# One graph-attention layer on one core: batches of eight tiles, E times Q made with features on partitions, and every edge tile gathered

## The chip, the cores and the metric

The kernel runs on one core of a Trainium2 chip. A core has five engines that each run their own queue of instructions in order: TensorE (PE: matmuls; PEld: its weight loads), VectorE (DVE), ScalarE (ACT), GpSimd (POOL) and SyncE (SP). They wait for each other through semaphores. SyncE starts the plain transfers between the device memory (HBM) and the on-chip memory (SBUF); GpSimd starts the indirect ones, which fetch rows by a list of indices. Results of TensorE go to PSUM, a small memory of eight banks, and are read from there by VectorE and ScalarE. The metric is device time in microseconds (us) of one execution. A short program on the host only lays the inputs out (transposed copies, padded index lists).

## The reference

There are 6250 nodes with 128 features, eight heads of 16 features, and 206,250 edges sorted by their destination node. For every edge e from `src` to `dst`:

```
Q = x @ WQ;  K = x @ WK;  V = x @ WV        # per node, 128 wide
E = edge_attr @ WE                          # per edge, 128 wide
score[e,h] = sum over the head's 16 features of K[src] * Q[dst] * E[e]
w[e,h]     = exp(clip(score / 4, -5, 5))
out[n]     = sum over edges into n of w * V[src]  /  (sum of w + 1e-6)
result     = layernorm(x + out)
```

Everything is float32. Three tensors meet in the score: K by a random source node, Q by a destination that hardly moves from edge to edge, and E by the edge itself.

## The kernel before

The edges are cut into 1612 tiles of 128. Four tiles make a batch (`B = 4`; a few smaller batches at the end).

**Tables.** `table` (from L256) computes K and V of all nodes as one row of 256 numbers and stores them to HBM (`kv`). `q_rows` (L284) makes Q as three bfloat16 parts and stores it (`qs`); `load_q` (L308) loads the 42 destination rows that a group of eight tiles can need. Until the table is stored, the first 12 batches (`XB`, 48 tiles) gather rows of x and `project` (L408) turns them into K and V: transposes, a copy, matmuls, copies.

**Gathers.** `gather` (L388) issues one indirect transfer per tile: 128 rows of 1 KB into `kvrows` (L397, GpSimd). There are 14 buffers of four tiles. From batch 18 on (`LOCK`) the first gather of a batch also waits for a matmul of TensorE several batches earlier (`lag`, `expanded`): the gathers are tied to TensorE's pace.

**Column tiles.** For two batches in five, from batch 32 on, the last tile is not gathered: 146 tiles in all (`column_tiles`, L74). `columns` (L352) copies, for each of the tile's 128 edges, one column of the transposed x (4 bytes on each of 128 partitions) into `xcol`, at an address that the engine loads into a register (L365, L370): 96 copies on ScalarE and 32 on VectorE per tile. `project_columns` (L372) multiplies the tile by the K and V weights and `place_columns` (L382) copies the result to where a gather would have put it.

**A batch's way.** `stage_a` (L457): TensorE expands Q of the destinations into `qps` with a one-hot matrix (L464: edges on the output's partitions, the one-hot is the stationary operand, so one weight load per tile), and multiplies the edge features with WE into `eps` (L469, again one weight load per tile). `stage_b` (L472): VectorE multiplies K by Q (L475), the product by E (L478), sums over 16 features (L481) and clips (L484). `weigh` (L487): ScalarE takes the exponential twice, into PSUM for the multiplication (L490, `exp_p`) and into the message (L492). `messages` (L517): VectorE multiplies V by the weights (L519). `stage_c` (L524): TensorE sums the messages into windows of nodes with a second one-hot (L541, `agg`); ScalarE copies finished windows out (L552), `finish` (L507) adds the windows of 256 nodes up (`finps`, L504), and `layernorm` (L735) runs in pieces on VectorE between other work (`fill`).

**Order.** One loop over the batches (L585) emits `stage_a` of batch b, `stage_b` of b-1, `messages` and `stage_c` of b-2. From batch 12 on that order is kept as written (a manual schedule); before that the framework's scheduler orders the instructions. SyncE's queue carries the edge features (`ea`, L334), the broadcast destinations (`relb`, L324), `qw`, `xb` and the results.

Of the kernel before, what the change touches and what calls it, by code (L numbers as in the profile page):

```python
# [16 lines left out]
P = 128  # L17
# [3 lines left out]
B = 4  # L21
G = 4
# [7 lines left out]
GB = 14  # L30
XB = 12
LOCK = XB + 6
STEP = 3
GLEAD = 2
OHB = 5
# [5 lines left out]
AHEAD = 2  # L41
EB = 6
SLAG = 2
# [8 lines left out]
COL0 = 32  # L52
COLP = (5, 2)
COLA = (8, 12)
COLV = (8, 4)
COLL = 8
RING = 4096
SUMS = 8
XT_AT = RING + P
# [3 lines left out]
def cut_batches():  # L63
    out, t = [], 0
    while t < NT:
        k = B
        if t >= NT - TAIL:
            k = 2 if NT - t > 3 else 1
        out.append(range(t, t + k))
        t += k  # L70
    return out


def column_tiles():  # L74

    batches = cut_batches()
    at = (COL0 + k * COLP[0] // COLP[1] for k in range(len(batches)))
    return [batches[b][-1] for b in at if b < len(batches) and batches[b][-1] < NT - TAIL - 4 * B]

# [22 lines left out]
def edge_attention(ctx: ExitStack, tc: tile.TileContext, x, xT, srcT, srcC, dstT, dstB, dst0, bnd, lo, eaT,  # L102
# [26 lines left out]
    onehots = [cp.tile([P, HW + 2 * B * P], F32, name=f"onehot{i}") for i in range(OHB)]  # L129
# [4 lines left out]
    col_batches = [t // B for t in column_tiles()]  # L134
    col_half = (len(col_batches) + 1) // 2
    col_at = cp.tile([col_half, 2, P], I32, name="col_at")
# [4 lines left out]
    with ExitStack() as fast:  # L141
# [80 lines left out]
        def count_inside():  # L222

            W = 4 * 2 * D
            for a in range(0, NT, W):
                e = min(NT, a + W)
                cl = wp.tile([P, W], F32, name="cl", tag="kvst", bufs=2)[:, :e - a]
                count(P, cl, rel[:, a:e], HW - 1)
            nc.vector.tensor_reduce(cn[:, :1], cn, axis=AX.X, op=ALU.add)
            pc = psT.tile([1, 1], F32, name="pc", tag="oT")  # L230
            nc.tensor.matmul(pc, cn[:, :1], ones, start=True, stop=True)
            nc.vector.tensor_copy(cnt_i, pc)
# [7 lines left out]
        psT = fast.enter_context(tc.tile_pool(name="psT", bufs=2, space=bass.MemoryType.PSUM))  # L240
        psA = fast.enter_context(tc.tile_pool(name="psA", bufs=2, space=bass.MemoryType.PSUM))
        psX = fast.enter_context(tc.tile_pool(name="psX", bufs=1, space=bass.MemoryType.PSUM))

        iota_p = psX.tile([P, HW], F32, name="iota_p")
        exp_p = psX.tile([P, B, H], F32, name="exp_p")
        nc.vector.tensor_copy(iota_p, iota_f[:, :HW])

        def pair_bank(i, name, shape):

            pool, tag = ((psE, "eps"), (psT, "oT"), (psQ, "qps"), (psT, "oT"))[i % 4]  # L250
# [33 lines left out]
        def q_rows(q):  # L284
            n = min(P, N - q * P)
            ps = psT.tile([P, D], F32, name="qrows", tag="oT")
# [40 lines left out]
        chunks, aggs, sums, st8, expanded = {}, {}, {}, {}, {}  # L327
# [15 lines left out]
        def lag(b):  # L343

            return max(STEP, 12 - (b - LOCK) // 40)

        col_tiles, xT_bytes = {}, xT_sb.bitcast(U8)
        used = [0]

        copied, projected = {}, []  # L350

        def columns(eng, b, share=1.0):  # L352

            size, runs = COLA if eng is nc.scalar else COLV
            first = 0 if eng is nc.scalar else COLA[0] * COLA[1]
            engine = mybir.EngineType.Activation if eng is nc.scalar else mybir.EngineType.DVE
            copy = eng.copy if eng is nc.scalar else eng.tensor_copy
            due = int((b - COL0 + COLL - 1 + share) * runs * COLP[1] / COLP[0] + 1e-6)
            while copied.get(engine, 0) < min(due, len(col_batches) * runs):
                k, j = divmod(copied.get(engine, 0), runs)  # L360
                copied[engine] = copied.get(engine, 0) + 1
                if k not in col_tiles:
                    col_tiles[k] = wp.tile([P, P], F32, name="xcol", bufs=4)
                to, j = col_tiles[k].bitcast(U8), first + j * size
                at = nc.values_load_multi_w_load_instructions(  # L365
                    col_at[k % col_half:k % col_half + 1, k // col_half, j:j + size], engines=(engine,),
                    min_val=XT_AT + 4 * LEFT, max_val=XT_AT + 4 * (LEFT + N - 1),
                    skip_runtime_bounds_check_because="edges name nodes")[1]
                for c in range(size):
                    copy(to[:, 4 * (j + c):4 * (j + c) + 4], xT_bytes[:, ds(at[c] - XT_AT, 4)])  # L370

        def project_columns(b):  # L372

            if b not in col_batches:
                return
            g = gathered[b]
            k = col_batches.index(b)
            pk = psT.tile([P, 2 * D], F32, name="colkv", tag="oT")
            nc.tensor.matmul(pk, col_tiles.pop(k), wkv_sb, start=True, stop=True)  # L379
            projected.append((g, pk))  # L380

        def place_columns():  # L382

            while projected:
                g, pk = projected.pop()
                nc.vector.tensor_copy(g[:, B - 1, :], pk)

        def gather(b, made=None):  # L388
            rows, f = (x, D) if b < XB else (kv, 2 * D)
            g = gp.tile([P, B, 2 * D], F32, name="kvrows")  # L390
            for i, t in enumerate(batches[b]):
                if b in col_batches and i == B - 1:
                    continue
# [6 lines left out]
                if i == 0 and b >= LOCK:  # L400
                    made = expanded[b - lag(b)]
# [6 lines left out]
        def project(g, n):  # L408

            pt = psT.tile([P, B, P], F32, name="xtps", tag="oT")  # L410
            for i in range(n):
                nc.tensor.transpose(pt[:, i, :], g[:, i, :D], ident)
            xgT = wp.tile([P, B, P], F32, name="xgT", tag="kq", bufs=2)
            nc.scalar.copy(xgT[:, :n], pt[:, :n])
            for i in range(0, n, 2):
                k = min(2, n - i)
                pk = pair_bank(i // 2, "kvps", [P, 2, 2 * D])
                for j in range(k):
                    nc.tensor.matmul(pk[:, j, :], xgT[:, i + j, :], wkv_sb, start=True, stop=True)  # L419
                nc.scalar.copy(g[:, i:i + k, :], pk[:, :k, :])  # L420

        def together(b):

            t0 = batches[b][0]
            n = len(batches[b])
            if n == B and b + 1 < nbat and len(batches[b + 1]) == B and t0 % (2 * B) == 0:
                return [b, b + 1]
            return [] if n == B and t0 % (2 * B) else [b]

        def stage_0(b):  # L430
            group = together(b)
            if not group:
                return
            t0, n = batches[b][0], sum(len(batches[i]) for i in group)
            tl = onehots[used[0] % OHB]
            used[0] += 1
# [3 lines left out]
            for i in group:  # L440
                st8[i] = tl, HW + (batches[i][0] - t0) * P - HW * pair_of(batches[i][0])[1], None

        def stage_0t(b):
            group = together(b)
            if not group:
                return
            t0, n = batches[b][0], sum(len(batches[i]) for i in group)
            ohT = wp.tile([QROWS, 2 * B * P], BF16, name="onehotT", bufs=3)
# [3 lines left out]
            for i in group:  # L452
                tl, at, _ = st8[i]
                k = (batches[i][0] - t0) * P
                st8[i] = (tl, at), ohT[:, k:k + len(batches[i]) * P]

        def stage_a(b, g):  # L457
            t0, n = batches[b][0], len(batches[b])
            if b < XB:
                project(g, n)  # L460
            oh, ohT = st8.pop(b)
            pq = psQ.tile([P, B, D], F32, name="qps")
            for i in range(n):
                expanded[b] = nc.tensor.matmul(pq[:, i, :], ohT[:, i * P:i * P + P], loaded[t0 // WT],  # L464
                                               start=True, stop=True)
            pe = psE.tile([P, B, D], F32, name="eps")
            ea = ea_tiles(t0, n)
            for i in range(n):
                nc.tensor.matmul(pe[:, i, :], ea[:, i * P:i * P + P], we_sb, start=True, stop=True)  # L469
            st8[b] = [n, g, oh, pq, pe]  # L470

        def stage_b(b):  # L472
            n, g, oh, pq, pe = st8[b]
            t0 = wp.tile([P, B, D], F32, name="kq", bufs=2)
            nc.vector.tensor_tensor(t0[:, :n], g[:, :n, :D], pq[:, :n], op=ALU.mult)  # L475
            yield
            t1 = wp.tile([P, B, D], F32, name="kqe", bufs=2)
            nc.vector.tensor_tensor(t1[:, :n], t0[:, :n], pe[:, :n], op=ALU.mult)  # L478
            yield
            sc = wp.tile([P, B, H], F32, name="sc")  # L480
            nc.vector.tensor_reduce(sc[:, :n], t1[:, :n].rearrange("p b (h d) -> p b h d", h=H),  # L481
# [3 lines left out]
            st8[b] = [n, g, oh, sc]  # L485
# [327 lines left out]
```

## Time and profile before

| | |
|---|---|
| three runs | 2565.03, 2586.32, 2592.5 us (median 2586.32) |
| the profiled execution | 2567.26 us, of which 2565.4 us are the span from its first to its last instruction |
| mean granted TensorE clock | 0.75 of full speed |
| busy: PE / PEld | 1624.0 us (63%) / 1407.1 us (55%) |
| busy: VectorE, ScalarE, GpSimd | 1843.5 us (72%), 1644.0 us (64%), 1396.9 us (54%) |
| indirect gathers | 1466 (48 from x, 1418 from `kv`) |
| DMA | 380.81 MB, mean 148 GB/s |

How to read the profile's rows: "L370 ACT COPY xcol<-xT_sb 128x4 uint8 x14016 | 1499.0, 189 | 573.0 <-issue 560.3" is a group of 14,016 copies of line 370 on ScalarE that write `xcol` from `xT_sb`; together they were busy for 1499.0 us, one lasts 189 ns (they overlap a little), and the engine stood idle for 573.0 us just before them, 560.3 of it while it waited for nothing that the profile shows ("issue"). In a timeline the first two numbers are start and duration in us, and the bracket is the idle time before. "remote" is a wait ended by a semaphore that the profile can't assign.

### The profile page before, as it was taken

To read this page: it belongs to the slowest core of one execution; us is meant where nothing else is said; L and a number is where in the kernel's file an instruction comes from. 1 tells how busy PE (TensorE), PEld (TensorE's weight loads), DVE (VectorE), ACT (ScalarE), POOL (GpSimd) and SP (SyncE) were. 2 spreads that over 40 slices of the span, in tenths; PEclk is the share of its full clock that TensorE was granted. 3 is DMA by queue.
4 is the path that set the end of the run, shared out by engine and by line. 5 is a ranking of instruction groups with operands and counts; after the bars stand their busy time and mean duration, and the time that the engine had idled before them with its cause. 6 is when DMAs were issued, how large, how long until landed. Compare 5 with 4: busy or idle time off the path is not lost.

```text
span 2565.4 us, 49832 instructions
## 1 busy us (share of the span) xinstructions
PE 1624.0 (63%) x9342; PEld 1407.1 (55%) x9342; DVE 1843.5 (72%) x8070; ACT 1644.0 (64%) x15015; POOL 1396.9 (54%) x1473
## 2 busy tenths in 40 slices
PE   5656566676666666666666655667666656566665
PEld 3446555565665555555555555556556555455555
DVE  2436678878777777777767777877877777777786
ACT  1211667777776677676767767777776666776760
POOL 6446555555555455555554555555655555555564
PEclk7777777777776777776777768777876777777787
DMA  7545445645554464455444544564654455545542
GB/s 233 153 130 179 136 125 157 176 134 169 153 148 132 134 176 138 123 147 174 130 135 136 175 140 129 147 175 137 183 147 126 136 144 164 145 131 144 173 145 79
DMA packets 171028, 380.81 MB, mean 148 GB/s; under 512 B 58653, under 2 KB 84569, under 8 KB 170707
## 3 DMA queue, kind: packets, MB, share of 16 engines
q0 software_dynamic: 69584, 189.03, 25.8%
q1 hardware_dynamic: 99983, 187.46, 24.4%
q14 instruction: 244, 2.00, 0.2%
q8 instruction: 77, 1.26, 0.2%
q10 hardware_dynamic: 1140, 1.06, 0.1%
HBM read 362.61 MB, written 14.81 MB: 147 GB/s over the span
## 4 chain that ended last, share of the span: by engine, by line
ACT 46%; issue 25%; DVE 11%; PE 8%; ACTq 6%; another core or an unknown queue 3%; DMA 1%; DVEq 0%; SPq 0%
ACT xcol L370 42%; ACTq L365 6%; DVE xcol L370 2%; PE agg L541 2%; PE eps L469 2%; ACT msg L492 2%; DVE kqe L478 2%; DVE msg L519 1%; DVE kq L475 1%; PE finps L504 1%; ACT exp_p L490 1%; PE kvps L419 1%; DVE sc L481 1%; ACT sum L552 1%
## 5 line engine op out<-in xcount | busy, mean ns | idle before, releaser
L397 POOL DMA_INDIRECT kvrows<-kv,src x1418 | 1350.3, 952 | 1120.4 <-PE qps L464 420.4
L370 ACT COPY xcol<-xT_sb 128x4 uint8 x14016 | 1499.0, 189 | 573.0 <-issue 560.3
L541 PE MATMUL agg<-msg,onehot 128*128 128x136 f32 x3224 | 639.1, 358 | 441.3 <-DVE msg L519 316.8
L541 PEld LDWEIGHTS agg<-msg,onehot 128*128 128x128 f32 x3224 | 562.4, 254 | 492.2 <-ACT msg L492 276.5
L469 PE MATMUL eps<-we_sb,ea 128*128 128x128 f32 x3224 | 599.6, 343 | 164.5 <-DVE kqe L478 95.3
L469 PEld LDWEIGHTS eps<-we_sb,ea 128*128 128x128 f32 x3224 | 517.8, 244 | 220.6 <-DVE kqe L478 128.7
L519 DVE TENSOR_TENSOR msg<-kvrows,exp_p 128x512 f32<-128x512 f32 x406 | 275.9, 679 | 488.8 <-ACT exp_p L490 276.4
L370 DVE COPY xcol<-xT_sb 128x4 uint8 x4672 | 410.9, 192 | 30.2 <-issue 23.0
L464 PE MATMUL qps<-qw,onehotT 126*128 126x128 bf16 x1612 | 193.5, 254 | 240.7 <-DVE kq L475 163.2
L464 PEld LDWEIGHTS <-onehotT 126*128 126x128 bf16 x1612 | 154.7, 117 | 325.3 <-issue 306.8
L478 DVE TENSOR_TENSOR kqe<-kq,eps 128x512 f32<-128x512 f32 x406 | 274.6, 676 | 52.3 <-remote 30.7
L475 DVE TENSOR_TENSOR kq<-kvrows,qps 128x512 f32<-128x512 f32 x406 | 273.7, 674 | 37.5 <-remote 21.3
L481 DVE TENSOR_REDUCE sc<-kqe 128x32 f32<-128x512 f32 x406 | 272.8, 672 | 5.8 <-DVE y L761 0.5
L490 ACT ACTIVATE exp_p<-sc 128x32 f32<-128x32 f32 x406 | 78.3, 193 | 139.7 <-DVE sc L484 76.8
L437 DVE TENSOR_TENSOR onehot<-iota_p,dst_sb 128x512 f32<-128x512 f32 (+2 forms) x206 | 137.6, 669 | 11.0 <-remote 9.0
L379 PE MATMUL colkv<-wkv_sb,xcol 128*128 128x256 f32 x292 | 127.9, 533 | 0.0
L504 PE MATMUL finps<-sum,shift 128*128 128x136 f32 x640 | 95.2, 310 | 17.1 <-ACT sum L552 11.1
L504 PEld LDWEIGHTS finps<-sum,shift 128*128 128x128 f32 x640 | 91.1, 219 | 19.6 <-ACT sum L552 13.1
L492 ACT ACTIVATE msg<-sc 128x32 f32<-128x32 f32 x406 | 87.2, 215 | 22.2 <-issue 21.7
L450 DVE TENSOR_SCALAR onehotT<-relb,node 126x1024 bf16<-126x1024 bf16 (+2 forms) x206 | 99.8, 485 | 1.8 <-DMA relb<-relD 1.7
L484 DVE TENSOR_SCALAR sc<-sc 128x32 f32<-128x32 f32 x406 | 83.7, 206 | 4.2 <-issue 3.8
L379 PEld LDWEIGHTS colkv<-wkv_sb,xcol 128*128 128x128 f32 x292 | 69.1, 285 | 0.0
(73 smaller groups left out, 568.9 us busy)
## 6 DMA issues: line engine op xcount, KB each, us to landing
ea<-eaT SPq DMA_DIRECT2D x201, 512.0 KB
relb<-relD SPq DMA_DIRECT2D x100, 504.0 KB
kvrows<-kv,src POOLq DMA_INDIRECT x1418
qw<-qs SPq DMA_DIRECT2D x202, 31.5 KB
kv<-kvst SPq DMA_DIRECT2D x12, 512.0 KB
qs<-qst SPq DMA_DIRECT2D x48, 96.0 KB
xb<-x SPq DMA_DIRECT2D x24, 128.0 KB
out<-h SPq DMA_DIRECT2D x24, 128.0 KB
```

The lines of the kernel that those rows point to most:

```text
L365: at = nc.values_load_multi_w_load_instructions(col_at[k % col_half:k % col_half + 1, k // col_half, j:j + size], engines=(engine,), min_v ...
L370: copy(to[:, 4 * (j + c):4 * (j + c) + 4], xT_bytes[:, ds(at[c] - XT_AT, 4)])
L379: nc.tensor.matmul(pk, col_tiles.pop(k), wkv_sb, start=True, stop=True)
L397: ins = nc.gpsimd.indirect_dma_start(out=g[:k, i, :f], out_offset=None, in_=rows, in_offset=bass.IndirectOffsetOnAxis(ap=src_col(t)[:k], a ...
L464: expanded[b] = nc.tensor.matmul(pq[:, i, :], ohT[:, i * P:i * P + P], loaded[t0 // WT], start=True, stop=True)
L469: nc.tensor.matmul(pe[:, i, :], ea[:, i * P:i * P + P], we_sb, start=True, stop=True)
L475: nc.vector.tensor_tensor(t0[:, :n], g[:, :n, :D], pq[:, :n], op=ALU.mult)
L478: nc.vector.tensor_tensor(t1[:, :n], t0[:, :n], pe[:, :n], op=ALU.mult)
L481: nc.vector.tensor_reduce(sc[:, :n], t1[:, :n].rearrange("p b (h d) -> p b h d", h=H), axis=AX.X, op=ALU.add)
L504: nc.tensor.matmul(ps, shift[:, P - s:2 * P - s], sums[k // 2][:, k % 2], start=first and i == 0, stop=stop and i == len(parts) - 1)
L519: nc.vector.tensor_tensor(m[:, :n, :D].rearrange("p b (h d) -> p b h d", h=H), g[:, :n, D:].rearrange("p b (h d) -> p b h d", h=H), exp_p[ ...
L541: nc.tensor.matmul(aggs[u][:, 0 if final else k % 2], oh[0][:, oh[1] + i * P:oh[1] + i * P + P], m[:, i, :], start=not final and t % (2 * ...
```

## The change

The column tiles go, with all their copies and matmuls; each of the 1612 tiles is gathered. The gathers no longer wait for TensorE: a gather waits only for a free buffer (and, in the first part, for the table). A batch has eight tiles, there are eight gather buffers of eight tiles, and six batches (the same 48 tiles) are gathered from x.

The product of E and Q is made in transposed form. `stage_a` now has features on the output's partitions and 512 edges on its columns: the Q rows and WE are the stationary operands, loaded once per 512 edges. ScalarE copies the expanded Q to SBUF (`qT`), VectorE multiplies it by E in PSUM (`product`), TensorE turns the product back with eight transposes (`turn`), and VectorE multiplies it by K (`stage_b`). So VectorE still has four passes over a batch's 128 numbers per edge. The PSUM tiles are larger and single: `qps`, `eps` and the turned product `pps` take two banks each, the window sums share a bank with `exp_p`, and `qrows`, `finps` and `iota_p` share one.

```diff
-B = 4
+B = 8
-GB = 14
-XB = 12
-LOCK = XB + 6
-OHB = 5
+GB = 8
+XB = 6
+OHB = 3
...
         def gather(b, made=None):
             for i, t in enumerate(batches[b]):
-                if b in col_batches and i == B - 1:
-                    continue
...
-                if i == 0 and b >= LOCK:
-                    made = expanded[b - lag(b)]
...
+        def stage_a(b):
+            t0, n = batches[b][0], len(batches[b])
+            if b < XB:
+                project(gathered[b], n)
+            ohT = st8.pop(b)
+            ea = ea_tiles(t0, n)
+            pq = psQ.tile([P, B * P], F32, name="qps")
+            pe = psE.tile([P, B * P], F32, name="eps")
+            for i in range(0, n * P, G * P):
+                j = min(n * P, i + G * P)
+                nc.tensor.matmul(pq[:, i:j], loaded[t0 // WT], ohT[:, i:j], start=True, stop=True)
+            for i in range(0, n * P, G * P):
+                j = min(n * P, i + G * P)
+                nc.tensor.matmul(pe[:, i:j], we_sb, ea[:, i:j], start=True, stop=True)
+            qT = wp.tile([P, B * P], F32, name="eq", bufs=2)
+            nc.scalar.copy(qT[:, :n * P], pq[:, :n * P])
+            st8[b] = [n, qT, pe]
+
+        def product(b):
+            n, qT, pe = st8[b]
+            nc.vector.tensor_tensor(qT[:, :n * P], qT[:, :n * P], pe[:, :n * P], op=ALU.mult)
+            st8[b] = [n, qT]
+
+        def turn(b):
+            n, eq = st8[b]
+            pp = psP.tile([P, B, D], F32, name="pps")
             for i in range(n):
...
+                nc.tensor.transpose(pp[:, i, :], eq[:, i * P:i * P + P], ident)
+            st8[b] = [n, pp]
+
+        def stage_b(b, g):
+            n, pp = st8[b]
+            t0 = wp.tile([P, B, D], F32, name="kq", bufs=1)
+            nc.vector.tensor_tensor(t0[:, :n], g[:, :n, :D], pp[:, :n], op=ALU.mult)
             yield
...
+            nc.vector.tensor_reduce(sc[:, :n], t0[:, :n].rearrange("p b (h d) -> p b h d", h=H),
                                     axis=AX.X, op=ALU.add)
```

The order of one turn of the loop in the changed kernel, engine by engine: VectorE runs K times the turned product of b-1, `product` of b, the transposed one-hot of b+1, the sum over features of b-1, the messages of b-2, the clip of b-1 and the one-hot of b-1, with pieces of the layer norm and of Q's rows between them. TensorE runs the eight transposes of b, two matmuls of Q and two of E for b+1, the matmuls that add windows up where there are any, and the window sums of b-2. ScalarE runs the copy of Q for b+1, the two exponentials of b-1 and the copy of the window's sums. `project` keeps its steps but takes four tiles at a time through the banks that `qps`, `eps` and `pps` use.

More of the change, by code (lines that the diff above doesn't have):

```diff
@@ L71, in cut_batches @@
     return out
[L74 to L78, printed above, removed]
 def pair_of(t):
@@ L341, in ea_tiles @@
             return chunks[t // CH][:, j:j + n * P]
[L343 to L386, printed above, removed]
         def gather(b, made=None):
@@ L408, in project, with one_hots @@
         def project(g, n):
[L410 to L436, printed above, removed]
+            for a in range(0, n, G):
+                h = min(G, n - a)
+                pt = psP.tile([P, G, P], F32, name="xtps", tag="pps")
+                for i in range(h):
+                    nc.tensor.transpose(pt[:, i, :], g[:, a + i, :D], ident)
+                xgT = wp.tile([P, G, P], F32, name="xgT", tag="kvst", bufs=2)
+                nc.scalar.copy(xgT[:, :h], pt[:, :h])
+                for i in range(0, h, 2):
+                    k = min(2, h - i)
+                    pk = pair_bank(i, "kvps", [P, 2, 2 * D])
+                    for j in range(k):
+                        nc.tensor.matmul(pk[:, j, :], xgT[:, i + j, :], wkv_sb, start=True, stop=True)
+                    nc.scalar.copy(g[:, a + i:a + i + k, :], pk[:, :k, :])
+        def one_hots(b):
+            t0, n = batches[b][0], len(batches[b])
+            tl = onehots[b % OHB]
             nc.vector.tensor_tensor(tl[:, HW:].rearrange("p (t n) -> p t n", n=P)[:, :n, :HW],
@@ L439, in stage_0, with turned_one_hots @@
                                     rel[:, t0:t0 + n, None].to_broadcast([P, n, HW]), op=ALU.is_equal)
[L440 to L448, printed above, removed]
+        def turned_one_hots(b):
+            t0, n = batches[b][0], len(batches[b])
+            ohT = wp.tile([QROWS, B * P], BF16, name="onehotT", bufs=2)
             e0 = t0 % RC * P
@@ L451, in stage_0t @@
                                     op0=ALU.is_equal)
[L452 to L457, printed above, removed]
+            st8[b] = ohT
+        def stage_a(b):
             t0, n = batches[b][0], len(batches[b])
             if b < XB:
-                project(g, n)
-            oh, ohT = st8.pop(b)
-            pq = psQ.tile([P, B, D], F32, name="qps")
-            for i in range(n):
[L464 to L470, printed above, removed]
@@ L548, in stage_c @@
                         fill()
[L549 to L553 removed]
+                    norms.append(layernorm(nc, sp, agg[:, u % 2:u % 2 + 1], xbs.pop(QL), out, QL, 1, stores))
+                elif tail:
+                    sums[k] = sp.tile([P, MW], F32, name="sum", bufs=SUMS)
+                    nc.scalar.copy(sums[k], agg[:, k % 2])
+                    while len(finished) < QL // 2 and all(v <= k for v, _ in windows(2 * len(finished) + 1)):
                         ready.append(len(finished))
[L555 to L557 removed]
+                        finished.append(k)
+        gathered = {0: gather(0)}
         for b0 in range(0, NB, KB):
@@ L562, in edge_attention @@
             for b in range(len(gathered), min(XB, nbat)):
-                if (b - 2 if b < 5 else b) * KB > b0:
+                if (2 * b - 1 if b < 3 else 2 * b + 1) * KB > b0 and b0 + KB < NB:
                     break
@@ L614, in edge_attention @@
             pending.clear()
+            steps = stage_b(b - 1, gathered.pop(b - 1)) if 0 <= b - 1 < nbat else iter(())
+            next(steps, None)
+            if b < nbat:
+                product(b)
+            fill()
+            if b + 1 < nbat:
+                turned_one_hots(b + 1)
+            fill()
+            if b < nbat:
+                turn(b)
+            if b + 1 < nbat:
+                stage_a(b + 1)
+            next(steps, None)
+            fill()
+            if 0 <= b - 2 < nbat:
+                messages(b - 2)
+            fill()
+            next(steps, None)
+            if 0 <= b - 1 < nbat:
+                weigh(b - 1)
+                one_hots(b - 1)
+            fill()
             for j in ready:
```

131 lines of the change are left out of this document (39 added, 92 removed).

## The prediction

> **What bounds the kernel now.** I read four views in this order: the chain that ended last, the groups of instructions, the timeline of GpSimd in a stretch of the middle, and the timeline of TensorE there.
>
> ```profile
> ACT 46%; issue 25%; DVE 11%; PE 8%; ACTq 6%; another core or an unknown queue 3%; DMA 1%; DVEq 0%; SPq 0%
> ...
> L397 POOL DMA_INDIRECT kvrows<-kv,src x1418 | 1350.3, 952 | 1120.4 <-PE qps L464 420.4
> L370 ACT COPY xcol<-xT_sb 128x4 uint8 x14016 | 1499.0, 189 | 573.0 <-issue 560.3
> ...
> L519 DVE TENSOR_TENSOR msg<-kvrows,exp_p 128x512 f32<-128x512 f32 x406 | 275.9, 679 | 488.8 <-ACT exp_p L490 276.4
> ...
> L478 DVE TENSOR_TENSOR kqe<-kq,eps 128x512 f32<-128x512 f32 x406 | 274.6, 676 | 52.3 <-remote 30.7
> ```
>
> The chain is ScalarE's: its column copies and the "issue" time around them. The second group says why: 1499.0 us busy and 573.0 us idle around the copies are 2072 us of the 2565.4. The copies delay the exponential, and VectorE's messages wait 276.4 us for it. GpSimd is idle for 1120.4 us in front of its gathers, most of it for TensorE, to which they are tied: it follows, it doesn't lead.
>
> ```profile
> 1203.00 0.94 POOL L397 DMA_INDIRECT kvrows<-kv,src  x1 [6.31 <-PE qps L464]
> 1204.25 0.95 POOL L397 DMA_INDIRECT kvrows<-kv,src  x1 [0.30 <-issue]
> 1205.50 0.94 POOL L397 DMA_INDIRECT kvrows<-kv,src  x1 [0.30 <-issue]
> 1206.74 0.94 POOL L397 DMA_INDIRECT kvrows<-kv,src  x1 [0.30 <-issue]
> ```
>
> When nothing holds it, GpSimd starts a gather every 1.25 us: 0.95 of work and 0.30 that is always there. This number carries the prediction.
>
> **Part by part.** The time counts from the profiled execution (2565.4 us span, 2567.26 us), which is 19 us under the median of the three runs; a time set by GpSimd should move less than those runs do.
>
> *Gathers.* 1466 become 1612, and their wait for TensorE goes. At 0.952 mean plus 0.30 they take 1612 x 1.252 = 2018 us if nothing holds them: 10.0 us per batch of eight. Everything else must fit under 10.0 us per batch, or it becomes the bound. Before took 2565.4/201.5 = 12.7 us per eight tiles.
>
> *ScalarE.* The 14,016 copies go. Added: one copy of 128x1024 from PSUM per batch; a copy of 128x512 (`xgT`) takes 585 ns, so it costs between 0.59 and 1.17 us; I take 1.0. With two exponentials of 64 instead of 32 per partition (0.2 each, from 193 and 215 ns) and a sum copy (0.27 at 128x136) ScalarE works about 1.8 us per batch.
>
> *VectorE.* The 4672 copies and 146 placing copies go. Still four passes per batch, now 1024 wide. The passes take 676 ns at 512, `h<-h,xb` takes 419 at 256, so about 1 ns per element and 1.19 us each; the bounds are 1.00 (`cl`, 128x1024) and 1.35 (twice 676). Four are 4.8 us. The one-hots stay (0.67 and 0.49 per eight tiles), the clip is 0.2, and layer norm and Q's rows are 177 us in all, 0.9 per batch. Sum 7.0 us, with 0.5 for gaps 7.5.
>
> *TensorE.* Its rows come in two speeds, because the granted clock alternates:
>
> ```profile
> 1203.34 2.08 PE L469 MATMUL eps<-we_sb,ea 128*128 128x128 f32 x8 [0.61 <-DVE kqe L478]
> 1205.20 2.02 PE L541 MATMUL agg<-msg,onehot 128*128 128x136 f32 x8
> ...
> 1207.74 0.39 PE L464 MATMUL qps<-qw,onehotT 126*128 126x128 bf16 x4
> 1207.96 1.11 PE L469 MATMUL eps<-we_sb,ea 128*128 128x128 f32 x8
> 1208.91 1.09 PE L541 MATMUL agg<-msg,onehot 128*128 128x136 f32 x8
> ```
>
> Per eight tiles, fast and slow: `eps` 2.2 and 4.2 at most. A 512-column matmul isn't in the trace; it streams the same columns with fewer weight loads, so it can only be shorter, and 256-column `kvps` (four in 1.08 and 2.07 us) point to 1.9 and 3.6. I take 2.1 and 4.1, near the measured rows. `qps` 0.6 and 1.2, `agg` 2.2 and 4.2, windows and Q rows 0.5 and 1.0. New are eight transposes: four `xtps` took 0.60 and 1.06 us, so 1.0 and 2.0. Sum 6.4 us fast, 12.5 slow; with the mean durations of before (clock 0.75) 9.3. At 6.4 it is under GpSimd's 10.0, at 12.5 it is over.
>
> The new loop is `product` of b (1.2), transposes, `qps`, `eps` of b+1, then `product` of b+1: 1.2 + 1.0 + 0.6 + 2.1 = 4.9 us fast, 8.5 slow, plus hand-offs of 0.1 to 0.2. The single PSUM tiles therefore don't close a loop longer than 10 us by themselves: the window sums run while VectorE does K times the product. Where TensorE falls behind, the gathers are up to six batches (48 tiles) ahead, so only the mean counts.
>
> *DMA.* The queues were busy 25.8% (gathers, 189 MB) and 24.4%. With 146 more gathers that is about 1370 us of 2125, 64%, at 190 GB/s; the first slice ran at 233 GB/s. GpSimd waited only 2.8 us in all for earlier gathers to land. I count nothing; if landings became late, `stage_b` would wait for them, not GpSimd.
>
> *Start and end.*
>
> ```profile
> 198.03 0.94 POOL L397 DMA_INDIRECT kvrows<-kv,src  x1 [16.38 <-PE eps L469]
> ...
> 2543.74 0.90 POOL L397 DMA_INDIRECT kvrows<-kv,src  x1 [1.10 <-PE qps L464]
> ```
>
> The gather of 198.03 is the 105th; at 1.25 us each it would have started at 134, so the start cost 64 us over the first gather's 3.6. The same things rule the start after: 48 gathers from x, the table (first `kv` gather at 80.4), then buffers that come free only as the first batches are projected. Before projected its 48 tiles from 81.5 to 164, 13.4 us per eight. After, `project` shares its banks with `qps`, `eps` and `pps`, so a batch is a chain: `product` 1.4, transposes 1.2, K times product 1.3, then twice (transposes 0.6, copy 0.7, `kvps` 2.1, copies 0.8) 8.4, `qps` and `eps` 1.5, copy 1.2: 15.0 us. That is 10 us more over six batches, and the stall of 16 us for late index loads stays. Start: 64 + 10 + 3.6 = 78. From the last gather to the end it was 21.7 us; I keep 22.
>
> Sum: 78 + 2018 + 22 = 2118, and 2 us around the span: 2120. Between 200 and 260 us before's VectorE stood idle six times for 2.4 to 6.0 us, in part on waits that the profile can't assign ("remote"); I add 5 us for a slow stretch there. **Forecast 2125 us**, 17% under before.
>
> [...] One gather is long:
>
> ```profile
> 221.59 2.29 POOL L397 DMA_INDIRECT kvrows<-kv,src  x1 [0.30 <-DVE sc L484]
> ```
>
> It started beside a VectorE instruction of 1.69 us that works from SBUF to SBUF (`dst_sb`, L209). [...]
>
> **The rivals.**
>
> *TensorE becomes the bound at a mixed or low clock.* For it: 9.3 us per batch at the clock of before is close to 10.0, and TensorE also shows idle time without a visible cause. Against it: in a busy stretch (120 to 140 us) the clock was 0.98, so a TensorE that is behind speeds up. Price: 11 us per batch give 100 + 201.5 x 11 = 2317; the slow sum of 12.5 less the 0.5 to 0.6 that wider matmuls save, 11.9, gives 2498. I expect 2180 to 2400. [...]
>
> *Slower than before: the half clock stays and the hand-offs show.* The mechanism is one: TensorE works each batch in order at half clock, 12.5 us, and VectorE and ScalarE find their inputs late by the unassigned waits of before (136 us on the three `kq`, `kqe` and `msg` groups, 0.7 us per eight tiles). It decides from 12.25 us per batch ((2565.4 - 100)/201.5 = 12.24); 12.5 + 0.7 gives 100 + 201.5 x 13.2 = 2760. Against it: it needs a low clock at 100% busy, which the rows don't show.
>
> *The change doesn't do what it says:* the gathers still wait, now for buffers. They do at the start; later only if a batch takes more than 10.0 us, which is the first rival.
>
> *Faster than the forecast:* the start overlaps and costs 40 us instead of 78: 2085. Below lies only the floor of 2018.
>
> **How the numbers follow.** GpSimd's pace (2085 to 2180): 0.64. TensorE at a mixed clock (2180 to 2400): 0.22. TensorE slower still, 2400 to 2541: 0.05. Slower than before: 0.07. Within 1%, which is what a measurement of this kernel can tell from no change: 0.02. Range 2080 to 2390, which leaves out 0.14 and a little at its ends. Faster by over 1%: 0.91.
>
> **What would show it.** Right: gathers 1.25 us apart for nearly the whole span, GpSimd busy near 72% (1535 us), VectorE idle before K times the product and waiting for gathers; ScalarE under 25%. The term of the transposes is right if eight take 1.0 to 2.0 us, of the wide passes if they take 1.2. Wrong: GpSimd idle for VectorE's messages (a buffer not free) in the middle of the span, TensorE over 85% busy, a batch's period over 10.3 us, or the first free-running gather later than 230 us.

## The result: slower, by 3.6%

The changed kernel takes 2673.43 us (median of four runs, 2666.96 to 2679.62) and the kernel before 2581.77 us beside it: a ratio of 1.0361, 95% interval 1.0297 to 1.0425. 2125 us were forecast. The profiled execution took 2679.62 us, 2677.8 of them the span.

The chain of work that ended last and the costliest groups of the changed kernel's page:

```profile
another core or an unknown queue 40%; PE 26%; issue 13%; DVE 10%; POOL 4%; ACT 3%; DMA 2%; DVEq 1%; SPq 0%; ACTq 0%; POOLq 0%
...
L334 POOL DMA_INDIRECT kvrows<-kv,src x1564 | 1493.4, 955 | 1077.4 <-DVE sc L413 568.9
L467 PE MATMUL agg<-msg,onehot 128*128 128x136 f32 x3224 | 565.0, 340 | 763.1 <-ACT agg L419 564.4
...
L448 DVE TENSOR_TENSOR msg<-kvrows,agg 128x1024 f32<-128x1024 f32 (+2 forms) x206 | 245.9, 1194 | 693.0 <-ACT sum L478 648.8
...
L478 ACT COPY sum<-agg 128x136 f32<-128x136 f32 x201 | 54.9, 273 | 1358.2 <-remote 853.0
```

The column copies are gone as planned, but no engine is busy for more than 58% of the span: GpSimd is idle for 1077 us in front of its gathers (450 of them are the 0.30 us that each gather has ahead of it), VectorE for 693 us in front of its messages. Each row points on to the next. GpSimd waits for VectorE to free a buffer; VectorE's messages wait for ScalarE's copy of the window sums (L478); that copy waits 853 us for something the profile calls "remote", and 40% of the chain is that. Who it is shows in a stretch of the timeline (gathers, transfers and other rows left out; GpSimd issued 16 gathers without a break from 1161.6 to 1181.5 us):

```profile
1168.67 2.02 PE L467 MATMUL agg<-msg,onehot 128*128 128x136 f32 x16
...
1171.57 1.09 PE L401 MATMUL pps<-ident,eq 128*128 128x128 f32 x8 [0.88 <-issue]
...
1172.50 0.60 PE L384 MATMUL qps<-onehotT,qw 126*128 126x512 bf16 x2
...
1172.93 1.88 PE L387 MATMUL eps<-ea,we_sb 128*128 128x512 f32 x4
...
1184.53 0.27 ACT L478 COPY sum<-agg 128x136 f32<-128x136 f32 x1 [15.86 <-remote]
1184.70 1.02 ACT L389 COPY eq<-qps 128x1024 f32<-128x1024 f32 x1
1184.84 1.22 DVE L448 TENSOR_TENSOR msg<-kvrows,agg 128x1024 f32<-128x1024 f32 x1 [11.80 <-ACT sum L478]
```

TensorE's window sums have their recorded end, which the profile models, at 1170.7 us, and the copy that needs nothing else starts at 1184.5. The trace also keeps the moments at which TensorE's semaphore rose: 1184.46, 1184.55, 1184.59 and 1184.65. Four signals in 0.19 us, for sums, transposes, Q and E, whose matmuls start one after the other over 4 us from 1168.67 on: the last three signals at least were held back, long after their matmuls had started. Whether the signal itself is held or the last writing of the results, the trace doesn't tell. The profile couldn't match a release 14 us after the end, and said "remote".

How late such signals are depends on how long GpSimd has been gathering without a break. The next table is worked out from the starts and recorded ends in the trace (after 300 us): for every instruction of VectorE or ScalarE that waits for TensorE, how long after TensorE's recorded end it was held with nothing else in its way, by the time from the start of the run of gathers to that end (a run is gathers with only the usual 0.30 us between them).

```
age of the run of gathers, us     0-2   2-4   4-6   6-8   8-10  10-12  no run
mean lateness, us                 0.02  0.12  0.68  2.93  6.45  4.56   0.17
share over 1 us late              0%    0%    17%   52%   61%   38%    4%
```

83 of the 99 runs there are 16 gathers long, two batches. So gathering and computing take turns: some 5 to 8 us into a run most signals stop, the other engines stand still, GpSimd fills its buffers and has to stop, the signals come, two batches pass quickly and free two buffers. A batch takes 12.87 us.

A second fact is needed to read the experiments. The kernel before was timed beside each group of them and took 2544 to 2575 us with three groups, and 1944 to 1949 us with four others; one chip number appears on both sides. I call the two the **slow** and the **quick condition**, whatever lies behind them. The first measurement is of the slow one.

### The profile page after: what moved, and what is told of

Its sections match the earlier page's. It is cut to its first block, busy times and chain, and to the rows that moved or that the text cites. A ratio compares the mean times of both kernels' runs of the same rounds, so it can differ in the third digit from the quotient of the medians.

```text
span 2677.8 us, 22505 instructions
## 1 busy us (share of the span) xinstructions
PE 1456.3 (54%) x7044; PEld 1101.6 (41%) x7044; DVE 1326.0 (50%) x2247; ACT 363.6 (14%) x905; POOL 1540.0 (58%) x1619
## 4 chain that ended last, share of the span: by engine, by line
another core or an unknown queue 40%; PE 26%; issue 13%; DVE 10%; POOL 4%; ACT 3%; DMA 2%; DVEq 1%; SPq 0%; ACTq 0%; POOLq 0%
PE agg L467 10%; PE pps L401 5%; PE eps L387 5%; POOL kvrows L334 4%; DVE eq L394 2%; PE qps L384 2%; DVE kq L407 2%; PE bank L433 2%; DMA kvrows<-kv,src 2%; DVE msg L448 2%; PE kvps L356 1%; ACT agg L419 1%; PE kvacc L246 1%; DVE onehot L362 1%
## 5 line engine op out<-in xcount | busy, mean ns | idle before, releaser
L334 POOL DMA_INDIRECT kvrows<-kv,src x1564 | 1493.4, 955 | 1077.4 <-DVE sc L413 568.9
L448 DVE TENSOR_TENSOR msg<-kvrows,agg 128x1024 f32<-128x1024 f32 (+2 forms) x206 | 245.9, 1194 | 693.0 <-ACT sum L478 648.8
L401 PE MATMUL pps<-ident,eq 128*128 128x128 f32 x1612 | 263.7, 316 | 305.2 <-DVE eq L394 215.3
L387 PE MATMUL eps<-ea,we_sb 128*128 128x512 f32 (+1 forms) x812 | 411.5, 629 | 0.7 <-issue 0.6
L401 PEld LDWEIGHTS pps<-ident,eq 128*128 128x128 f32 x1612 | 221.7, 166 | 334.7 <-issue 265.1
L394 DVE TENSOR_TENSOR eq<-eq,eps 128x1024 f32<-128x1024 f32 (+2 forms) x206 | 245.9, 1194 | 200.2 <-remote 113.1
L407 DVE TENSOR_TENSOR kq<-kvrows,pps 128x1024 f32<-128x1024 f32 (+2 forms) x206 | 245.6, 1192 | 92.5 <-remote 54.5
L389 ACT COPY eq<-qps 128x1024 f32<-128x1024 f32 (+2 forms) x206 | 205.0, 995 | 500.5 <-PE qps L384 234.9
L410 DVE TENSOR_REDUCE sc<-kq 128x64 f32<-128x1024 f32 (+2 forms) x206 | 243.6, 1182 | 0.1
L478 ACT COPY sum<-agg 128x136 f32<-128x136 f32 x201 | 54.9, 273 | 1358.2 <-remote 853.0
L387 PEld LDWEIGHTS eps<-ea,we_sb 128*128 128x128 f32 x812 | 168.2, 208 | 146.8 <-issue 111.8
L334 POOL DMA_INDIRECT kvrows<-x,src x48 | 45.7, 951 | 23.7 <-issue 13.4
```

Source lines behind the costliest of these rows:

```text
L334: ins = nc.gpsimd.indirect_dma_start(out=g[:k, i, :f], out_offset=None, in_=rows, in_offset=bass.IndirectOffsetOnAxis(ap=src_col(t)[:k], a ...
L387: nc.tensor.matmul(pe[:, i:j], we_sb, ea[:, i:j], start=True, stop=True)
L389: nc.scalar.copy(qT[:, :n * P], pq[:, :n * P])
L394: nc.vector.tensor_tensor(qT[:, :n * P], qT[:, :n * P], pe[:, :n * P], op=ALU.mult)
L401: nc.tensor.transpose(pp[:, i, :], eq[:, i * P:i * P + P], ident)
L407: nc.vector.tensor_tensor(t0[:, :n], g[:, :n, :D], pp[:, :n], op=ALU.mult)
```

## The experiments

**The tie taken from the kernel before.**

```diff
-                if i == 0 and b >= LOCK:
-                    made = expanded[b - lag(b)]
```

> The kernel before, with one thing taken away: its gathers are no longer tied to TensorE, they wait only for a free buffer. Theory A (TensorE's completion signals reach the other engines late while GpSimd gathers without a break for more than about 5 us, so gathering and computing take turns): the signals are late along the whole span instead of in its first 300 us, and the time rises to 2620 to 2800 us. Theory B (the changed kernel is slow because its own loop through single PSUM tiles takes 13 us, and the gathers only follow): nothing bad happens here, 2540 to 2600 us.

> The kernel before without the tie of its gathers to TensorE, as the first experiment, for the chip of this call. Where before takes about 2550 us, theory A (long runs of gathers make TensorE's signals late): signals late along the whole span, 2600 to 2800 us. Theory E (the signals are late on such a chip whenever much is under way, gathers or not, and the tie has nothing to do with it): within 1% of before. Where before takes 1946 us: 1932 us as measured.

In the slow condition 2681.94 us against 2575.29: 1.0421 (1.0358 to 1.0485). That is theory A's number, and theory E (within 1%) falls; but theory A's mechanism is borne out only in part. After the first 300 us TensorE's signals are late for 194 us in all, spread over the whole span, against 39 us in the kernel before. Yet the runs of gathers did not get longer: 302 of 350 are of three or four gathers, against 280 of 337 before, since a free gather waits for its buffer, for VectorE's messages (815.9 us). So the length of a run is not the whole condition; why the untied gathers delay more at the same length stays open. In the quick condition 1931.78 against 1945.91: 0.9925 (0.9897 to 0.9954), and after the first 200 us no signal of TensorE is late. The gathers and ScalarE's column copies, first in the slow condition, then in the quick one:

```profile
L397 POOL DMA_INDIRECT kvrows<-kv,src x1418 | 1353.5, 954 | 1208.0 <-DVE msg L517 815.9
L370 ACT COPY xcol<-xT_sb 128x4 uint8 x14016 | 1510.2, 190 | 653.7 <-issue 641.5
```

```profile
L397 POOL DMA_INDIRECT kvrows<-kv,src x1418 | 1354.1, 955 | 464.7 <-issue 342.9
L370 ACT COPY xcol<-xT_sb 128x4 uint8 x14016 | 1420.6, 189 | 69.0 <-issue 59.4
```

The same instructions, as long as before, but 654 us of idle time around ScalarE's copies in the one and 69 in the other. So most of the "issue" time that I read as ScalarE's own cost belongs to the same disturbance. The kernel before, in the slow condition, by its copies' starts (means, us):

```
age of the run of gathers, us        0-2    2-4    4-6    6-8    8-12   3 to 5 us after its end
from one column copy to the next     0.108  0.133  0.392  0.596  0.573  0.108 us
the same, quick condition, no tie    0.127  0.133  0.121  0.133  0.116
```

**The tie given to the changed kernel.** Once per batch (on the transposes of the batch four before) or twice (also on the window sums of the batch six before):

```diff
...
+                if i == 0 and b - LAG in turned:
+                    made = turned[b - LAG]
+                if i == B // 2 and b - LAG - 2 in summed:
+                    made = summed[b - LAG - 2]
...
```

> The changed kernel, with the first gather of each batch tied to TensorE again: it waits for the eight transposes of the batch four before it. Theory A: runs of 16 gathers (20 us) become runs of 8 (10 us) with breaks, TensorE's signals are late less often, 2200 to 2500 us. Theory B: no gain, 2650 to 2700 us.

> As the run before, but the fifth gather of each batch also waits for TensorE, for the window sums of the batch six before it: runs of four gathers (5 us). Theory A: lateness nearly gone, 2100 to 2350 us, faster than with runs of eight. Theory B: 2650 to 2700 us.

> The changed kernel with two ties to TensorE in each batch of eight gathers, for the chip of this call. Where before takes about 2550 us, theory A: runs of four gathers, signals mostly on time, 2150 to 2450 us. Theory E: 2600 to 2700 us. Where before takes 1946 us: 2114 us as measured.

In the slow condition, two ties: 2462.32 us, 0.9568 of before (0.9513 to 0.9623) and 8% under the changed kernel, the one version here that beats both there. The gain is real but theory A's range was missed: the runs shrank only to 4 to 16 gathers (9.5 on average against 14.4), presumably because the ties too hang on late signals, and the signals are still late:

```profile
L335 POOL DMA_INDIRECT kvrows<-kv,src x1564 | 1492.2, 954 | 867.9 <-issue 416.8
```

A batch takes 11.73 us, with 5.67 us of lateness in front of ScalarE's instructions, against 12.85 and 6.50 without ties. In the quick condition one tie gives 2111.67 us and two 2113.73, 8.5% and 8.6% over before: what binds there is shown below. That 2113.73 lies in the range set for theory A is luck, since no signal is late there. Four ties a batch, and one batch later:

> The changed kernel with four ties to TensorE in each batch of eight gathers, spread over its transposes, Q, E and window sums, and one batch later than in the run with two ties. Where before takes about 2550 us: if the length of an unbroken run of gathers decides, runs of two give less lateness and 2150 to 2400 us; if the mean load of gathers decides, 2440 us or more. Where before takes about 1946 us: 2100 to 2200 us, bound by the gathers or by waits for TensorE.

> The changed kernel with four ties to TensorE per batch of eight gathers. Where before takes about 2550 us: 2150 to 2400 us if the length of an unbroken run decides, 2440 us or more if the mean load decides. Where before takes 1946 us: 2122 us as measured.

2122.10 and 2125.64 us, both in the quick condition, where a tie only costs. For the slow one this stays untried.

**The gathers left out.**

```diff
...
+            if b > XB and len(batches[b]) == B and b < nbat - 1:
+                return kept[0]
...
```

(The kept rows take a place of their own, and the gather buffers are six instead of eight.)

> The changed kernel without most of its gathers: every full batch after the seventh reads the rows gathered for the seventh, so K and V of the wrong nodes are used; all else is done. Theory A: TensorE's signals are on time and a batch takes what VectorE and TensorE need, 8.5 to 10 us: 1800 to 2100 us. Theory B: the loop still takes 13 us: 2600 to 2680 us.

> The changed kernel in which full batches after the seventh read the rows gathered for the seventh (K and V of the wrong nodes), for the chip of this call. Where before takes about 2550 us, theory A: no late signals without gathers, close to the 1503 us of the other call, at most 1650 us. Theory E: late signals remain, 2000 us or more.

1503.24 us in the quick condition and 1519.76 in the slow one: without gathers the two are alike. A batch takes 6.8 us, after 400 us hardly a signal is late (2 us in all), and the chain is VectorE's; theory B, a loop closed by the single PSUM tiles, falls, and so does theory E, which wanted 2000 us or more. Theory A's own 1800 to 2100 us was missed as well: it had put the work of a batch at 8.5 to 10 us. The slow condition's chain:

```profile
DVE 69%; PE 16%; issue 8%; ACT 1%; DMA 1%; another core or an unknown queue 0%; SPq 0%; DVEq 0%; ACTq 0%
```

**The changed kernel again.**

> The changed kernel as it is, beside the kernel before, on the chip of this call. In the last call the kernel before took 1946 us instead of 2582 and no signal of TensorE was late after the first 200 us. Theory D (two causes: on the chip of the first measurement the late signals, elsewhere GpSimd's floor of 1612 gathers): where the kernel before takes about 1946 us, the changed kernel is gather-bound and takes 2085 to 2120 us, 7 to 9% slower than before, with GpSimd busy at 72% or more; where before takes about 2580 us, the changed one takes 2670 us with late signals. Theory A alone: late signals and about 2.4 to 4.5% slower on any chip.

> The changed kernel as it is, again beside the kernel before. Where the kernel before takes about 2550 us: 2630 to 2680 us with TensorE's signals late. Where before takes about 1946 us (the call of the four first experiments): bound by 1612 gathers of 1.25 us, 2085 to 2120 us, no late signals.

> The changed kernel as it is. Where before takes about 1946 us: bound by 1612 gathers, 2085 to 2120 us, 7 to 9% slower than before. Where before takes about 2550 us: 2640 to 2680 us as measured three times.

In the slow condition 2641.87 against 2543.77 us (1.0384) and 2674.11 against 2575.29 (1.0391). In the quick one 2093.55 against 1944.39: 1.0773 (1.0728 to 1.0818), slower too, but for another reason, as theory D (two causes) had it. Its chain and rows:

```profile
POOL 39%; issue 21%; DMA 19%; DVE 14%; PE 6%; ACT 1%; SPq 0%; DVEq 0%; ACTq 0%; POOLq 0%
...
L334 POOL DMA_INDIRECT kvrows<-kv,src x1564 | 1487.8, 951 | 512.5 <-issue 441.7
...
L407 DVE TENSOR_TENSOR kq<-kvrows,pps 128x1024 f32<-128x1024 f32 (+2 forms) x206 | 246.5, 1197 | 562.6 <-DMA kvrows<-kv,src 554.2
...
L478 ACT COPY sum<-agg 128x136 f32<-128x136 f32 x201 | 54.7, 272 | 496.3 <-PE agg L467 492.6
```

GpSimd hardly stops: 1604 of 1611 gathers follow the one before by 1.255 us, VectorE waits 554 us for their data, and "remote" is gone. This is the kernel that was forecast. It loses because before, with 146 gathers less, needs only 1944 us there.

**What of the gathers does it.** Plain transfers of the same rows' bytes, and gathers of half the bytes:

```diff
+                if b >= XB:
+                    r = t * P % (N - P)
+                    nc.sync.dma_start(g[:k, i, :], kv[r:r + k, :])
+                    continue
```

```diff
-            rows, f = (x, D) if b < XB else (kv, 2 * D)
+            rows, f = x, D
```

> The changed kernel with the indirect gathers from the K and V table replaced by plain transfers of SyncE: the same 128 rows of 1 KB into the same place per tile, but consecutive rows of the table, so the nodes are wrong. Where before takes about 2550 us: theory A1 (what makes TensorE's signals late is the indirect kind, written by GpSimd): signals on time, 1520 to 1750 us. Theory A2 (any transfers of this volume and number do it): signals late, 2300 us or more. Where before takes about 1946 us: 1520 to 1750 us with either.

> The changed kernel with all gathers taken from x instead of the K and V table: 1612 gathers of 128 rows, but 512 bytes a row instead of 1 KB; the messages use the same numbers as the scores, so K and V are not those of the node. Where before takes about 2550 us: theory V (the bytes in flight make the signals late): lateness mostly gone, 2090 to 2300 us, bound by GpSimd. Theory I (the issue of gathers, their number and their descriptors, does it): 2600 to 2690 us as with full rows. Where before takes about 1946 us: 2085 to 2120 us with either.

> The changed kernel with plain transfers of SyncE in place of the indirect gathers from the table (consecutive rows, so wrong nodes). Where before takes about 2550 us: theory A1 (the indirect kind makes TensorE's signals late) 1670 to 1750 us, near the 1670 us of the other kind of chip; theory A2 (any transfers of this volume) 2300 us or more.

> The changed kernel with all gathers from x, 512 bytes a row (wrong K and V). Where before takes about 2550 us: theory V (the bytes in flight) 2090 to 2300 us; theory I (number of gathers and their issue) 2600 to 2690 us. Where before takes 1946 us: 2089 us as measured.

All four fell in the quick condition: plain 1669.98 and 1662.35 us, half rows 2088.78 and 2092.11, against 2093.55 with full rows. Half the bytes take as long as all of them, so there the pace is set by GpSimd's issue and not by the bytes. The slow condition was reached with a kernel that holds all cases in one execution:

```diff
-            rows, f = (x, D) if b < XB else (kv, 2 * D)
+            rows, f = (x, D) if b < XB or 100 <= b < 150 else (kv, 2 * D)
...
+                if 50 <= b < 100 or b >= 150 and i % 2:
+                    r = t * P % (N - P)
+                    nc.sync.dma_start(g[:k, i, :], kv[r:r + k, :])
+                    continue
```

> The changed kernel in four stages: batches 6 to 49 gather full rows as it does; 50 to 99 take consecutive rows of the table by plain transfers of SyncE; 100 to 149 gather 512-byte rows of x; from 150 on every second tile is gathered in full, the others come by plain transfers (wrong nodes in all but the first stage). Read as us per batch of eight tiles. Where before takes about 2550 us: stage 1 takes 13.0 to 13.4. Theory A1 (the indirect kind, GpSimd's issue): plain 7.6 to 8.5 without late signals, half rows 12.5 to 13.4. Theory A2 (any traffic of this volume): plain 11 or more. Theory V (bytes): half rows 10.0 to 11. Half the gathers: 8 to 10 if late signals need long runs without a break, 10 or more if each gather costs its share. Where before takes about 1946 us: 10.1, 7.7 to 8, 10.1, 7.5 to 8.

> The same kernel in four stages, for the chip of this call. Where before takes about 2550 us, in us per batch of eight: stage 1 (full gathers) 13.0 to 13.4. Theory A1 (the indirect kind, GpSimd's issue): plain transfers 7.6 to 8.5, half rows 12.5 to 13.4. Theory A2 (any traffic of this volume): plain 11 or more. Theory V (bytes): half rows 10.0 to 11. Half the gathers: 8 to 10 if late signals need long runs, 10 or more if each gather costs its share. Where before takes about 1946 us: as in the run before.

The first of the two met the quick condition (1764.50 us), the second the slow one (2112.57 us). Busy time by stretch in the second: full gathers, plain transfers, half rows, half the gathers. The columns are start and end, length, then busy time and number of instructions of PE, PEld, DVE, ACT and POOL, the granted clock, DMA share and GB/s:

```profile
272.00:671.00 399.00, 219.44 (x1063) 165.28 (x1062) 210.71 (x353) 52.17 (x131) 235.39 (x247) 0.76 0.50 151
757.00:1052.00 295.00, 231.88 (x1278) 168.44 (x1279) 239.09 (x392) 64.56 (x156) 8.76 (x10) 0.93 0.88 252
1204.00:1684.00 480.00, 263.28 (x1290) 204.44 (x1289) 241.44 (x391) 62.21 (x157) 284.99 (x300) 0.77 0.37 111
1773.00:2052.00 279.00, 226.23 (x1290) 165.82 (x1289) 237.46 (x389) 63.73 (x157) 141.58 (x150) 0.96 0.91 269
```

VectorE does the same work in 295 us with plain transfers and in 480 us with half rows, while the plain stretch moves more than twice the bytes a second. By the starts of L398 (`product`) over 32 to 38 batches inside each stage, and the lateness in front of ScalarE's instructions:

```
us per batch of eight      full gathers   plain   half rows   half the gathers
slow condition             12.46          7.77    12.63       7.36
  of it late signals        6.28          0.19     6.31       0.93
quick condition             9.18          7.59     9.69       6.87
  of it late signals        0.00          0.00     0.00       0.00
```

Theory V (the bytes) and A2 (any traffic) fall; A1 holds: it is the indirect gathers as GpSimd issues them. Whether it is GpSimd's issuing or what the indirect transfers do afterwards, the runs don't separate. With half as many, 5 us to a batch and breaks between, 0.93 us of lateness is left. Not all of the forecasts were met: in the slow condition full gathers came out under 13.0 us and half the gathers under 8; in the quick one all four stages came out under theirs. For the full gathers the start explains it, where gathers had run ahead: the quick run of the changed kernel too took 9.0 us a batch in batches 12 to 45, and 10.0 after.

## Why the prediction was wrong

**The step that failed** is the last of "Start and end": "Between 200 and 260 us before's VectorE stood idle six times ... in part on waits that the profile can't assign ('remote'); I add 5 us for a slow stretch there." I took these waits for something of the start. They are what gathers without a break do to the other engines in the slow condition, and the start was the one place where before gathered long without a break (runs of 23, 24 and 19 gathers in its first 240 us). Worked out as in the table above, its signals were late for a third of the time from 20 to 300 us and for 1.7% of the time after: the trace before held the effect and its end, at the tie. The change made the start's way of working that of all 201.5 batches. In place of 5 us in all the runs showed 6.5 us of lateness a batch. It adds to the 6.8 us of work and not to the 10.0 us of gathers, so a batch took 12.87 us, and the term missing from the sum is about 2.9 us a batch, some 580 us: the changed kernel took 2673.43 us in the slow condition and 2093.55 in the quick one.

**Point by point.**

- *GpSimd's pace.* The pitch held (1.255 us when free) and so did 10.0 us per batch, where nothing disturbs: 2093.55 us in the quick condition against 2125. What was over-sized there is the start: the 105th gather started at 170.9 us, 37 us later than back-to-back gathers would have, not 74. (By the prediction's own rows, 81.5 to 164 us for six groups of eight tiles, before took 13.8 us for each, not 13.4.) In the slow condition it started at 196.7, 63 late.
- *The consumers' own work.* VectorE's 7.0 to 7.5 us per batch was good: 6.8 without gathers. The wide passes took 1.19 us each, ScalarE's copy 1.00, eight transposes 1.09 us at a granted clock of 1.00. E took 1.88 us at 1.00 and 3.61 at 0.52 where 2.1 and 4.1 were put, and TensorE, put at 9.3 us a batch with the durations of before, was busy 7.2 (1456.3 us in all). ScalarE's 1.8 us is what came (363.6 us in all), though its terms add up to 1.7.
- *"Where TensorE falls behind, the gathers are up to six batches ahead, so only the mean counts."* It fails in the slow condition: the buffers don't decouple two sides of which one stops while the other runs. 6.8 us of work and 6.5 of lateness follow each other almost wholly (13.3 together, 12.87 measured); the larger of 10.0 and 7.5 had been forecast.
- *What bounds before.* "The chain is ScalarE's" was right as a reading, but the 573 us of idle time around the copies were mostly no cost of the copies. Without the disturbance (and without the tie) they are 69 us, and before takes 1944 us. That number is under the floor of 2018 us for 1612 gathers: on such a run the change could not win at all, and nothing in the profile of before told me so.
- *The rival "slower than before"* named 0.07 and 2760 us. Its point of decision (12.25 us a batch) and its second half, the unassigned waits, are what came, at 0.7 us a batch instead of 6.5; its first half, the half clock, is not: the granted clock was 0.773, above before's 0.75.
- *"The change doesn't do what it says: the gathers still wait, now for buffers."* This came too, as a consequence: 568.9 us for VectorE's clip (L413), the instruction recorded last before the buffer's release, and bursts of 16. A buffer not free in the middle of the span and a batch over 10.3 us were two of the prediction's own signs of being wrong.
- *The long gather.* Beside the same instruction of VectorE (1.69 us, from 221.70 us) a gather of the changed kernel's profiled execution took 1.61 us. Beside `onehotT` the gathers are hardly longer: in the quick condition, after 300 us, the 190 that ran beside one took 0.971 us each against 0.947 for the others, and the pitch of 1604 free gathers is 1.255 us against the 1.252 assumed, 5 us in all.

TensorE and ScalarE were slowed in the slow condition alone. In the quick one TensorE's signals are 0.00 us late per batch and ScalarE's copies start 0.116 to 0.133 us apart at every age of a run; in the slow one the signals are 6.28 us late per batch with full gathers, and the copies start 0.39 to 0.60 us apart instead of 0.108 once a run of gathers is 4 us old. By what way the gathers reach these two engines no run shows.

## What to carry to other kernels

A wait that the profile can't assign is a row like any other: find out what was going on each time, and ask whether the change makes that condition the rule. Compare a consumer's start with its producer's recorded end; a semaphore that comes 14 us late looks like "remote" or "issue" and not like a wait for TensorE. Before a dependency is removed because the engine behind it looks idle, look in the trace for the stretch where it doesn't bind yet: here the first 200 us of before were the experiment.

## What the hardware showed that was not expected

- A run of indirect gathers of more than about 4 us slowed other engines in the slow condition: TensorE's signals came up to 17 us after the recorded ends, and ScalarE's copies went from one per 0.108 us to one per 0.4 to 0.6 us, at 0.108 again 3 to 5 us after the run. VectorE's signals were not late: in 131 batches of the changed kernel ScalarE's exponential started at most 0.4 us after VectorE's clip. The length of the run is not the whole condition, as the kernel before without its tie shows. Full rows and half rows do it alike (6.28 and 6.31 us a batch), plain transfers don't (0.19).
- The kernel before took 1944 us beside one group of runs and 2575 us beside another, and within a group its times lay within 0.5% of each other (1.1% in the first measurement). One chip number had both, 2543.77 and 1947.11 us. What the condition is, and what the gathers share with the signals, stays open.
- The traces of the slow condition lack records of semaphores. For the changed kernel the trace has 1389 of the 2216 signals of VectorE, 599 of ScalarE's 905 and 918 of TensorE's 1044; in the quick condition it has them all. They are missing during its runs of gathers: of VectorE's after 300 us, 247 of 258 are there in the first 2 us of a run and 106 of 329 at 6 to 8 us. VectorE's signals were in time all the same, so a missing record is not a late signal. But it shows that the gathers disturb the recording as well. Every run here was made with records of the span and the clock, so whether recording has a part in the late signals is a rival that no run rules out.
- A gather of 128 rows costs GpSimd 0.95 + 0.30 us with rows of 512 bytes as with rows of 1 KB, in both conditions: in the kernel with four stages 0.950 us for half rows and 0.953 for full ones in the slow one (GpSimd's 284.99 us for 300 instructions, 235.39 for 247), 0.948 for both in the quick one (278.71 for 294, 222.71 for 235).
